# Four graph layers on one core: preparation of layer 0 in three groups of rows, table roots, moved transposes, and another PSUM bank in layer 2

## The chip, the cores and the metric

The kernel runs on one core of a Trainium2 chip. The metric is the device time of one execution in microseconds (us). Times are given as the median of several runs. The profile shows one execution of its own, and all durations in this text come from it.

The engines of the core run beside each other, each through its own queue of instructions in order: TensorE (PE, with its weight loads PEld), VectorE (DVE), ScalarE (ACT), GpSimd (POOL) and SyncE (SP, here only for DMAs). An instruction that waits holds up all that is queued behind it on its engine.

## What is computed

x is 4096 rows of 64 numbers, adj a 4096x4096 matrix of zeros and ones with some 4 ones a row. Four layers follow, each of the form x = x + layer(h, adj), with h the layer-normalized rows of x cut at zero.

```python
def lorentz_linear(x, W, b, scale):
    h = x @ W.T + b
    time = sigmoid(h[:, :1]) * exp(scale) + 1.1
    xn = h[:, 1:]
    s = (time * time - 1.0) / clip(sum(xn * xn), 1e-08)
    return concatenate([time, xn * sqrt(s)])
# layer 0
h = lorentz_linear(h_in, W, b, scale); q = lorentz_linear(h, Wq, ...); k = lorentz_linear(h, Wk, ...)
att = adj * sigmoid((2 + 2 * (qm @ k.T)) / att_scale + att_bias)   # qm: q with its first column negated
support = att @ h;  out = support / sqrt(|inner product of support|)
# layer 1: out = w @ (h @ weight) + bias, w weighs each row's last 100 neighbours by powers of 0.5
# layer 2: out = 1 - 0.1 h - 0.01 sum(h * (adj @ h), 1)
# layer 3: out = relu([h, (adj @ h) / degree] @ W.T)
```

## The kernel before

**Tiling.** The 4096 rows lie as 32 tiles (`NT`) of 128 partitions. Sums are taken over 8 blocks (`NIB`) of 512 output rows; a block has 16 units (`NG`), each of two row tiles. The blocks of layer 0 run from 7 down to 0. `adjt` is read twice. Once it comes as masks: 128 loads on POOL's queue (`load_masks`, L175), one for each unit, which turn float32 into one byte and stay in SBUF for all four layers. Once it is read to check that it holds zeros and ones only (`check`, L355 and L352 on SP's queue, L356 on DVE). The checks are spread over the whole kernel as work between other work.

**Before layer 0's sums** (`before0`, `first_rows_and_block`, L500 to L1047). Rows are prepared in groups, `ROWS = ((16, 16), (0, 16))`: first row and count in tiles of 128. A group passes through a chain, in halves of 8 (`HR`). Mean (L532, DVE), centring (L539), squares (L544, ACT), variance (L549), reciprocal root (L554 and `newton`, L481: one start value and three steps of three instructions, all on DVE), product with the root (L558). Then it is transposed on PE (L580), copied on ACT (L595), multiplied with W on PE (L628; L620 adds the bias rows that `bias_rows` makes on POOL, L388 to L397), and copied out (L650). `factors` (L714) then takes the sigmoid of the first column (L664), squares (L673), norms (L698) and `ratio` (L704: three instructions around a `newton`). L745 writes the finished rows h into `fb`. The same again for q and k together: transposes, L628, copy L771, `factors` with twice the columns, L792 for k and q. k is transposed into `kt` (L580, L595), q in `queries_turned` (L859) and `queries_laid` (L869, four ACT copies into `qt`).

The order of all this on each engine, together with block 7's units, is set by a planner, `Listing` (L399). Every part has an engine, a cost in us, what it comes after, and at times a due time `at`. `plan` places the parts greedily; `run` tries 2500 random changes of priority and keeps one whenever the time of the last part is not longer than the best so far. The last part counts on every engine, the 40 mask loads on POOL included, of which load n (from 0) has the due time 2.2 * max(n - 5, 0). Where the plan has PE idle, `fill` puts in matmuls on nothing (L1039) of 0.215 us each, and 50 of them ahead of PE's first part.

**Layer 0's sums** (L1049 to L1101). Work goes in rounds of 4 units; the block after the first has rounds of 4, 4, 3 and 3 (`first`, L1068). In a round, each unit gets `scores` on PE (L920, into one of three PSUM tiles of two banks), `sigmoids` on ACT (L933), `masked` on DVE (L944), a mask load, perhaps a check, and one `step()` of the jobs that are queued (L307). After the units of the round, PE adds up the units of the round before (`gather`, L951). The first unit of a round of 4 writes its sigmoids to SBUF, which frees its PSUM tile; the others write in place, and the tile is free when DVE has read it. When a block is summed, `rows0` (L882) becomes a job: transpose on PE (L231, third step), copy on ACT (L237), then a long chain on POOL, ACT and DVE (root on POOL, L260 to L263) up to layer 1's rows (`norm`, L266, and `split`, L242). `queries(ib - 1)` (L874) transposes the next block's q at its seventh call, between the third and the fourth unit of a block's last round, and lays it out one unit later.

**Layers 1 to 3** (L1265 to L1536). Layer 1 counts on PE (L1235, L1245), turns counts into weights on ACT (L1261) and DVE (L1259) and multiplies (L1273). Layers 2 and 3 multiply the masks with the rows (L1345); every 4 products are one beat, with a `step()` and perhaps a check. `rows2` (L1385) is the job of a finished block of layer 2: copy out (L215), transpose (L231) into PSUM bank 3 (L1392), copy (L237), sums, normalization, transposes (L1410, bank 4), products with layer 3's weights (L1422) into banks 3 and 4, copies from there (L1430, L1431). The one-buffer PSUM tile "pr" of the pool `pm` serves the transposes of layer 0 and the products of `rows1` (L1146) in layer 1; in layer 3 it serves one small product (L1136).

## Time and profile before

| what | value |
|---|---|
| median of 3 runs | 599.48 us (599.21 to 599.6) |
| the profiled execution | 599.52 us, span 597.7 us, clock 0.997 |
| PE, DVE, ACT, POOL busy | 579.2, 484.2, 335.7, 238.5 us |
| first score matmul (L920) | at 49.32 us |
| end of block 7's sum | 84.25 us |
| end of block 6's sum | 118.2 us |
| end of layer 0 | 298.7 us |
| layer 2 from, layer 3 from | 461.1 us, 528.5 us |
| end | 597.7 us |

The span runs from the first to the last instruction; 1.8 us of the profiled execution lie around it. The page gives busy times; the chain of waits tells what released each step; the table by stage gives the busy time of each engine in a stretch; the timeline lists instructions in order, with the idle time before each and what ended it.

### The profile page before, as it was taken

The numbers are of one execution on the slowest core, as the hardware profiler recorded it, in microseconds if no ns is written. First come the engines' busy times: TensorE is split into PE (matmuls) and PEld (weight loads), VectorE is DVE, ScalarE is ACT, GpSimd is POOL, SyncE is SP. The second block draws the span as 40 slices with busy tenths as digits, with TensorE's granted clock in tenths as the row PEclk, the third lists the DMA queues.
The fourth block names the chain that finished last, engine by engine and source line by source line (L and its number), as shares of the span: only waits on it lengthen the run. The fifth ranks groups of instructions, "written<-read, shape, count | busy, mean of one in ns | idle before, by whom it ended". The sixth has DMA issues, their size and how long they took to land.

```text
span 597.7 us, 9243 instructions
## 1 busy us (share of the span) xinstructions
PE 579.2 (97%) x3135; PEld 237.4 (40%) x3135; DVE 484.2 (81%) x941; ACT 335.7 (56%) x541; POOL 238.5 (40%) x459
## 2 busy tenths in 40 slices
PE   8899999899999999899999999999998999899995
PEld 3563333233333333233343343343443544454553
DVE  5878677699999997999966878979887769987753
ACT  1568665767676765666527677767765014431221
POOL 7534204456767676744344401001010315462252
PEclk9999999999999999999999999999999999999998
DMA  9995902799999998973182545546556476546921
GB/s 140 145 105 43 105 10 20 77 141 148 161 153 162 148 154 154 133 149 98 43 316 73 177 155 193 164 158 192 163 177 200 152 253 205 169 148 193 322 85 42
DMA packets 43016, 87.04 MB, mean 146 GB/s; under 512 B 5136, under 2 KB 22032, under 8 KB 42960
## 3 DMA queue, kind: packets, MB, share of 16 engines
q1 hardware_dynamic: 23808, 68.40, 34.9%
q0 software_dynamic: 18720, 17.57, 31.6%
q10 hardware_dynamic: 432, 0.40, 0.3%
q8 instruction: 26, 0.43, 0.3%
q14 instruction: 30, 0.25, 0.1%
HBM read 135.63 MB, written 1.05 MB: 229 GB/s over the span
## 4 chain that ended last, share of the span: by engine, by line
PE 86%; DVE 5%; ACT 3%; issue 2%; POOL 2%; DMA 2%; ACTq 0%; DVEq 0%; POOLq 0%
PE acc L1345 19%; PE ps L920 17%; PE acc L951 17%; PE acc L1273 10%; PE cnt L1235 9%; PE cnt L1245 3%; PE many L1168 2%; PE pt L231 2%; PE idle L1039 2%; DVE att L944 1%; PE pr L1148 1%; DMA vec<-vecs_dram 1%; PE pn L1422 1%; ACT qt L869 1%; PE ps_q L628 1%
## 5 line engine op out<-in xcount | busy, mean ns | idle before, releaser
L356 DVE SCALAR_TENSOR_TENSOR ckw<-ckw 128x1024 f32<-128x1024 f32 x98 | 124.8, 1281 | 5.6 <-DMA ckw<-adjt_dram 5.3
L920 PE MATMUL ps<-qt,kt 64*128 64x512 f32 x512 | 125.2, 613 | 3.7 <-DVE att L944 3.4
L951 PE MATMUL acc<-att,fb 128*64 128x512 f32 x512 | 118.3, 600 | 0.0
L1261 ACT ACTIVATE w<-cnt 128x512 int16<-128x512 f32 x176 | 93.1, 597 | 42.8 <-PE cnt L1245 42.3
L944 DVE TENSOR_TENSOR att<-ps,mask 128x1024 f32<-128x1024 f32 x84 | 101.1, 1219 | 9.8 <-ACT ps L933 8.9
L933 ACT ACTIVATE ps<-ps,att_c,att_a 128x1024 f32<-128x1024 f32 x84 | 95.7, 1173 | 10.0 <-PE ps L920 6.9
L933 ACT ACTIVATE att<-ps,att_c,att_a 128x1024 f32<-128x1024 f32 x44 | 52.2, 1203 | 53.4 <-PE ps L920 52.8
L175 POOL DMA_DIRECT2D mask<-adjt_dram x128 | 70.2, 560 | 19.7 <-DMA mask<-adjt_dram 17.5
L920 PEld LDWEIGHTS ps<-qt,kt 64*128 64x128 f32 x512 | 44.1, 185 | 74.7 <-DVE att L944 21.4
L1259 DVE TENSOR_SCALAR w<-cnt 128x512 int16<-128x512 f32 x80 | 53.6, 686 | 22.9 <-PE cnt L1245 22.4
L944 DVE TENSOR_TENSOR att<-att,mask 128x1024 f32<-128x1024 f32 x44 | 56.0, 1288 | 17.2 <-ACT att L933 16.8
L1235 PE MATMUL cnt<-mask,after 128*128 128x512 fp8e4 x256 | 66.3, 379 | 2.1 <-DVE w L1259 1.6
L1273 PE MATMUL acc<-w,s2a 128*128 128x512 bf16 x256 | 66.5, 382 | 0.1
L951 PEld LDWEIGHTS acc<-att,fb 128*64 128x64 f32 x512 | 33.3, 136 | 79.4 <-issue 71.4
L275 POOL TENSOR_TENSOR xc<-x_sb,st 128x256 f32<-128x256 f32 x24 | 19.1, 794 | 108.5 <-DVE st L272 55.0
L1345 PE MATMUL acc<-mask,s2a 128*128 128x512 fp8e4 x256 | 57.8, 379 | 0.0
L1345 PE MATMUL acc<-mask,s2b 128*128 128x512 fp8e4 x256 | 57.7, 379 | 0.0
L260 POOL TENSOR_TENSOR rs_a<-rs_y 128x4 f32<-128x4 f32 x48 | 16.8, 351 | 81.4 <-DVE rs_y L256 72.2
L356 DVE SCALAR_TENSOR_TENSOR ck<-ck 128x512 f32<-128x512 f32 x60 | 44.9, 748 | 0.2 <-DMA ck<-adjt_dram 0.2
L1235 PEld LDWEIGHTS <-after 128*128 128x128 bf16 x256 | 24.8, 99 | 31.0 <-issue 3.4
L1345 PEld LDWEIGHTS <-s2b 128*128 128x128 f16 x256 | 25.0, 98 | 27.5 <-issue 0.8
L1345 PEld LDWEIGHTS <-s2a 128*128 128x128 f16 x256 | 24.6, 98 | 27.3
(196 smaller groups left out, 604.1 us busy)
## 6 DMA issues: line engine op xcount, KB each, us to landing
ckw<-adjt_dram SPq DMA_DIRECT2D x98, 512.0 KB, 3.4
mask<-adjt_dram POOLq DMA_DIRECT2D x128, 128.0 KB, 9.0
ck<-adjt_dram SPq DMA_DIRECT2D x60, 256.0 KB, 5.4
x_sb<-x_dram SPq DMA_DIRECT2D x4, 256.0 KB, 8.0
out_dram<-y POOLq DMA_DIRECT2D x6, 128.0 KB, 2.2
out_dram<-y ACTq DMA_DIRECT2D x2, 128.0 KB, 2.1
w_sb<-wts_dram SPq DMA_DIRECT2D x2, 80.0 KB, 7.7
vec<-vecs_dram ACTq DMA_DIRECT2D x1, 130.5 KB, 6.5
```

The source lines that it names most:

```text
L175: nc.gpsimd.dma_start(out=masks[ib][:, g * CG : (g + 1) * CG, :], in_=adjt[ib, g])
L275: nc.gpsimd.tensor_tensor(xc, xr, bc(st, CI), ALU.add)
L356: nc.vector.scalar_tensor_tensor(at, at, 0.0, at, ALU.not_equal, ALU.not_equal, accum_out=odd[:, k : k + 1])
L920: nc.tensor.matmul(ps[:, c, :], kt[half, g, :], qts[ib][half, :], start=True, stop=True)
L933: nc.scalar.activation(to, ps, AF.Sigmoid, bias=att_c, scale=att_a)
L944: nc.vector.tensor_tensor(att, frm, mask, ALU.mult)
L951: nc.tensor.matmul(acc[c * D : (c + 1) * D, :], lhs[:, t, :], rhs[:, c, :], start=(at == 0), stop=(at == NG - 1), skip_group_check=True,)
L1235: nc.tensor.matmul(cnt, after, masks[ib][:, t, :], start=True, stop=True, skip_group_check=True)
L1259: nc.vector.tensor_scalar(w, cnt, 0.0, None, ALU.max)
L1261: nc.scalar.activation(w, cnt, AF.Relu)
L1273: nc.tensor.matmul(accs[ib], both(s2a, t), w, start=(t == NT - 1), stop=False, skip_group_check=True,)
L1345: nc.tensor.matmul(acc, both(s2, t), masks[ib][:, t, :], start=(t == 0), stop=(t == NT - 1), skip_group_check=True,)
```

## The change

1. **Three groups.** `ROWS = ((24, 8), (8, 16), (0, 8))`, with start times of 6.6, 9.5 and 13.0 in the plan; `bias_rows` costs 8.1 there instead of 3.8. The queue of SP gets the first group's x (one DMA where there were two), the weights, then the other three x DMAs.
2. **Roots of the normalization** by ACT's Sqrt table (L285's form: one ACTIVATE for a group, then one reciprocal on DVE) instead of `newton`. A Sqrt on a spare number behind the Exp of the setup loads the table early. A Sigmoid on the same number comes after the Sqrt of all three groups, and all first sigmoids of h come after that.
3. **Roots in `ratio`** by `root`, a start value and two steps of mean form (reciprocal, product with a, sum) instead of `newton`'s three steps.
4. **Transposes at the end of a round.** `rows0` and `queries` wait, a step at a time, for the last unit of a round. For `queries` that is the end of a block's third round, three units earlier than before; for `rows0` one unit later. In rounds of 3 the first unit too writes its sigmoids to SBUF.
5. **`split`** of the last two blocks of layer 0 leaves four steps instead of two between its halves.
6. **Layer 2's transposed sums** go to the tile "pr" instead of bank 3.

```diff
+GUESS, SHARE = 515594453.0, 0.0624625
+    tried = cpool.tile([P, 1], F32, name="tried")
+    nc.scalar.activation(tried, exp_s[:, 0:1], AF.Sqrt)
...
-        ROWS = ((16, 16), (0, 16))
+        ROWS = ((24, 8), (8, 16), (0, 8))
...
-        def split(h, s2, rows):
+        def split(h, s2, rows, steps=2):
             nc.gpsimd.tensor_scalar(s2[:, rows, 0, :], h, 1.0 / STEP, None, ALU.mult)
-            yield
-            yield
+            for _ in range(steps):
+                yield
...
-        def newton(v, tag, m):
...
+        def root(y, a, tag):
+            z, q = (small(f"n{b}{tag}", "", pro, a.shape[1]) for b in "zq")
             nc.vector.tensor_scalar(
+                z.bitcast(I32), a.bitcast(I32), 0.5, GUESS, ALU.mult, ALU.add
             )
+            for share, to in ((SHARE, z), (0.25, y)):
+                nc.vector.reciprocal(q, z)
+                nc.vector.scalar_tensor_tensor(q, q, share, a, ALU.mult, ALU.mult)
+                nc.vector.tensor_tensor(to, q, z, ALU.add)
...
-            def roots(_):
-                nc.vector.tensor_scalar(v.va, v.va, 1.0 / D, EPS, ALU.mult, ALU.add)
-                v.rs = newton(v.va, f"x{gr}", R)
+            def rooted(_):
+                v.rs = numbers("rs")
+                nc.scalar.activation(v.rs, v.va, AF.Sqrt, bias=eps, scale=1.0 / D)
+            def inverted(_):
+                nc.vector.reciprocal(v.rs, v.rs)
...
-            at = (6.6, 14.5)[gr]
+            at = (6.6, 9.5, 13.0)[gr]
...
-            rs = add("DVE", 2.4, roots, *va)
+            sq = add("ACT", 0.25, rooted, *va)
+            tables.append(sq)
+            rs = add("DVE", 0.2, inverted, sq)
...
                     nc.vector.tensor_scalar(rr, rr, 1e-8, None, ALU.max)
-                    nc.vector.scalar_tensor_tensor(rr, t2, -1.0, rr, ALU.add, ALU.mult)
-                    y = newton(rr, f"{name}{gr}", R * n)
-                    nc.vector.scalar_tensor_tensor(rr, t2, -1.0, y, ALU.add, ALU.mult)
+                    nc.vector.reciprocal(rr, rr)
+                    nc.vector.scalar_tensor_tensor(t2, t2, -1.0, rr, ALU.add, ALU.mult)
+                    root(rr, t2, f"{name}{gr}")
...
-                return add("DVE", 2.8, ratio(name, n), tm, *rr)
+                return add("DVE", 2.25, ratio(name, n), tm, *rr)
...
         def queries(ib):
-            for _ in range(6):
+            for _ in range(3):
+                yield
+            while not edge[0]:
                 yield
             pt = pm.tile([P, CI, P], F32, tag="pr", name=f"pq_{ib}{sfx}")
...
             yield
-            yield
+            while not edge[0]:
+                yield
             pt = turned(asb, None, tag)
...
-            yield from split(h, s2a, rows)
+            yield from split(h, s2a, rows, 4 if ib < 2 else 2)
...
-            bias = add("POOL", 3.8, lambda _: bias_rows(), at=6.5)
+            bias = add("POOL", 8.1, lambda _: bias_rows(), at=6.5)
...
+            table = add("ACT", 1.5, lambda _: nc.scalar.activation(tried, tried, AF.Sigmoid), *tables)
+            for part in flats:
+                part.after += (table,)
+                table.then.append(part)
...
-                for ib, g in todo[k : k + size]:
+                for n, (ib, g) in enumerate(todo[k : k + size]):
+                    edge[0] = n == size - 1
                     ps = scores(ib, g)
-                    if size == 4 and not now:
+                    if size > 2 and not now:
...
+            edge[0] = True
...
-            pt = turned(asb, 3, tag)
+            pt = turned(asb, None, tag)
```

(`flats` holds each group's first ACT part of `factors` for h, the sigmoid L664.)

More of the change, by code (lines that the diff above doesn't have):

```diff
@@ L479, in run @@
                     part.emit(part)
-        def newton(v, tag, m):
-            y, a = (small(f"n{b}{tag}", "", pro, m) for b in "ya")
+        def root(y, a, tag):
+            z, q = (small(f"n{b}{tag}", "", pro, a.shape[1]) for b in "zq")
             nc.vector.tensor_scalar(
-                y.bitcast(I32), v.bitcast(I32), -0.5, 1597463007.0, ALU.mult, ALU.add
+                z.bitcast(I32), a.bitcast(I32), 0.5, GUESS, ALU.mult, ALU.add
             )
-            for _ in range(3):
-                nc.vector.tensor_tensor(a, y, y, ALU.mult)
-                nc.vector.scalar_tensor_tensor(a, a, -0.5, v, ALU.mult, ALU.mult)
-                nc.vector.scalar_tensor_tensor(y, a, 1.5, y, ALU.add, ALU.mult)
-            return y
+            for share, to in ((SHARE, z), (0.25, y)):
+                nc.vector.reciprocal(q, z)
+                nc.vector.scalar_tensor_tensor(q, q, share, a, ALU.mult, ALU.mult)
+                nc.vector.tensor_tensor(to, q, z, ALU.add)
+        tables, flats = [], []
         TURN = ("pm", "pa")
@@ L726, in factors @@
                 sg = add("ACT", 0.26, flat, *frm_parts)
+                if n == 1:
+                    flats.append(sg)
                 tm = add("DVE", 0.2 + 0.2 * n, time_sums(name, n, scales), sg)
@@ L852, in model @@
         spare, turn = [], [0]
+        edge = [False]
         qts = {}
```

## The prediction

> **What bounds the kernel now.** First the page's busy times. PE works almost all the time, so time is won only where PE idles, runs matmuls on nothing, or waits.
>
> ```profile
> PE 579.2 (97%) x3135; PEld 237.4 (40%) x3135; DVE 484.2 (81%) x941; ACT 335.7 (56%) x541; POOL 238.5 (40%) x459
> ```
>
> The average hides three stages, so I took the table by stage (us, then PE, PEld, DVE, ACT, POOL busy).
>
> ```profile
> 49.30:84.25 34.95, 34.83 (x150) 10.95 (x150) 26.00 (x34) 24.20 (x30) 10.89 (x17) 1.00 0.63 57
> 84.25:123.19 38.94, 37.06 (x164) 12.81 (x166) 28.38 (x47) 27.58 (x30) 18.35 (x48) 1.00 0.47 45
> 153.42:183.74 30.32, 30.32 (x136) 10.36 (x138) 28.38 (x48) 21.19 (x25) 20.91 (x46) 1.00 1.03 157
> 516.98:523.34 6.36, 5.84 (x36) 3.12 (x34) 6.09 (x14) 2.92 (x9) 2.95 (x5) 1.00 0.52 164
> ```
>
> From 49.3 us PE is full; before it, its work is mostly L1039, which is nothing. A block of layer 0 is full on PE at 30.3 us, with DVE behind it by 1.9 us only. Layer 2 has DVE at 6.09 of 6.36 us. Then I followed the first group's chain in the timeline.
>
> ```profile
> 12.06 0.34 DVE L554 TENSOR_SCALAR va<-va 128x16 f32<-128x16 f32 x1
> ...
> 15.08 0.69 DVE L558 SCALAR_TENSOR_TENSOR xc<-xc,nyx 128x512 f32<-128x512 f32 x1
> ...
> 22.54 1.28 ACT L664 ACT_TABLE_LOAD   x1
> ...
> 26.27 0.17 DVE L708 TENSOR_SCALAR rrh<-rrh 128x16 f32<-128x16 f32 x1
> ...
> 28.99 1.29 DVE L745 TENSOR_TENSOR fb<-t,rrh 128x512 f32<-128x512 f32 x2
> ```
>
> The normalization's root takes 3.0 us (12.06 to 15.08, fold's instruction and slow ones within), the ratio 2.7 us (26.27 to 28.99), the second ratio 2.9 us (41.02 to 43.95, 32 columns). The first score comes at 49.32.
>
> **Groups and roots: the start.** First the DVE sum. The two normalization roots go (3.0 and 2.3 us); three reciprocals of 0.2 us come: -4.7. A ratio was 13 instructions, at a step of 0.21 us (16 columns) or 0.225 us (32), and is now 10, three of them reciprocals. Rows for those: 0.17 us at 4 columns (L289), 0.25 at 16 (L1218), so some 0.007 us a column, 0.2 at 8 and 0.36 at 32. A ratio is then 2.1, 2.3 or 2.75 us at 8, 16 or 32 columns. But there are six of them instead of four: 2.1+2.3+2.1 for h and 2.3+2.75+2.3 for q and k, 13.9 against 11.2: +2.7. A third set of small instructions adds 1.0. DVE's 63.1 us up to 84.25 become some 62.1: its work hardly falls, only the first chain gets shorter.
>
> That chain, with 8 rows: mean from 7.6, centred 9.15, squares 9.85, variance 10.55, Sqrt (L285: 0.32) and reciprocal 11.15, normalized 11.85. There the gain stops for a while: PE's 50 matmuls on nothing end at 15.4, and the bias rows on POOL at 14.8. So transposed 16.05, copied 16.7, multiplied 18.1 (0.39 and 1.0), out at 18.75. The sigmoid must wait for the Sqrt of the third group: DVE is full from 7.6 with 3.0 us for the first group, 4.1 for the second, 2.2 for the third, so 17, and the table (1.28) is there at 18.5. Both meet. Sigmoid 19.0, squares 19.6, norms 20.3, ratio 22.4, rows 23.1, first column 23.3, transposed and copied 24.7, multiplied 26.2, out 27.3, sigmoid and squares 28.7, norms 29.4, ratio 31.7, k and q 33, q transposed and laid (1.5) and the other copy 35.5. With the other groups' instructions between I take the first score at 37 instead of 49.3.
>
> PE needed 34.9 us from there to the end of block 7's sum; 37 + 35 = 72. But the first group holds only 4 units (7.5 us of PE). The second group's k needs, in DVE's order, 46.5, the third's 65.6 with the masks between (1.25 us each): PE starves for 2 and 3 us. So 77 instead of 84.25: **-7.3 us**. DVE's idle time would fall from 13.8 (84.25 - 7.3 - 63.1) to 7.6 us. The planner speaks for the same place: its last mask load is due at 74.8 and costs 0.56, so no plan counts as better than 75.4 of its own us, and it has no reason to finish PE sooner. Bounds: 72 (nothing starves) and 82 (third group's k another 5 us late), -12 to -2.
>
> The added Sqrt table load is hidden: from 7.5, when Exp is done, to 8.8, ahead of the squares at 9.2; and PE is held until 15.4 anyway. The before shows 1.32 us from the end of the copy (22.51) to the sigmoid (23.83), the load within.
>
> The Trainium skill (ScalarE: Activation LUTs, What ACT_TABLE_LOAD costs) speaks against this edit: it gives 1.28 us for a load and 1.38 more for a drain at each switch. By it the Sqrt load would end at 10.2 and the sigmoid come 1.4 us later. The trace has the 1.28 and no drain, so I leave it out of the sum.
>
> On POOL, three halves of q instead of two (1.9 and 1.1 us) stand among the mask loads; masks came every 1.25 us from 21 us on, and 18 are enough by 60, so nothing waits. Price if it did: one load, 1.25.
>
> **Block 6 (84 to 123).** Its rounds without waiting are 2.2 us shorter than measured. The one long wait is PE from 111.9 to 113.5 for DVE, which came late because four qt copies (106.7 to 108.2) stood between ACT's sigmoids, and then the constants (110.6 to 112.2) on DVE. The copies now come a round earlier, where there are no checks, and the first unit of rounds of 3 goes to SBUF: **-1.6**, bounds -2.2 and 0.
>
> **Transposes at ends of rounds.** The chain of waits shows plain rounds and those with a transpose inside the scores:
>
> ```profile
> 153.42 3.58 PE acc L951 x16
> 157.00 3.63 PE ps L920 x16
> 160.64 3.58 PE acc L951 x16
> 164.22 2.78 PE ps L920 x12
> 167.37 1.06 PE ps L920 x4
> 168.42 3.58 PE acc L951 x16
> ```
>
> Sum to sum 7.22 us plain, 7.78 with q's two transposes (+0.56), 8.01 with the four of sums (+0.79). Once in the before q's stand at a round's end (100.46): there scores to sums took 3.14 against 2.77 (104.42), +0.37. So a place between is worth 0.19. Five q's and seven sums move: -2.3. Against it: the copies that follow now stand behind the first sigmoid of a round (qt 1.5 us, pt 0.59) where ACT was idle during the sums before. DVE then waits some 0.75 us for the second sigmoid in a round with three checks, and PE some 0.45 for DVE's fourth product, as DVE has only 1.9 us to spare in a block. Six blocks, half of them with such a wait: +1.3. **-1.0**, bounds -2.3 and +4.
>
> The wait near 237 (POOL's loads held for 2.1 us, then L275, then ACT) has no cause the profile names; I leave it, 2.2 either way. `split`'s two steps: the last block's chain has 20 steps of 23 before its rows are needed, so nothing.
>
> **Layer 2.**
>
> ```profile
> 508.74 0.71 PE L1422 MATMUL pn<-wxn_sb,ht 64*128 64x128 f32 x8
> ...
> 509.97 0.66 PE L231 MATMUL pt<-ident,asb 128*128 128x128 f32 x4 [0.52 <-ACT v L1431]
> ```
>
> Bank 3 holds pn until ACT has copied it, and pt waits. In the chain of waits that is 0.47 us, and pt takes 0.66 instead of 0.44 after a stop: 0.69 each, at 503.6, 510.0, 516.3 and 522.7: -2.8. "pr" is free: its last user in layer 1 is at 467, and sums follow each other by five beats. What is late next is DVE: 6.1 us of work in periods of then 5.7, 0.4 a period behind, 1.7 us in all, while its normalized rows (L297, done at 511.3) are now 1.8 us ahead of PE's use (513.06). **-2.3**, bounds -2.8 and -0.3.
>
> **Sum.** -7.3 - 1.6 - 1.0 - 2.3 = -12.2 on the profiled 599.52, which is the median within 0.04: 587.3. Between block 6 and layer 2 the work is tied to units, not to time, so an earlier start stays.
>
> **Rivals.**
> - *The start is bound by DVE after all* (its work does not fall; six ratios): block 7 ends at 82; 592.3. Chance 0.17.
> - *Nothing starves*: PE dense from 37, end at 72; 582.3. Against it: four units only in the first group. 0.15.
> - *Layer 2 is DVE's* (6.09 of 6.36 busy): -0.3 there, 589.3. 0.10.
> - *A table switch costs twice its row*: 1.28 more ahead of the first sigmoid, 588.6. The row speaks against it; beside it stands the page above. 0.05.
> - *Slower: ACT's detour reaches PE in full.* The two copies (2.09 us) and the check queued behind the late product (0.75) cost 2.84 a block, 17 us over six blocks, and block 6 gains nothing: 17 - 2.3 - 7.3 - 2.3 = +5, 604.6. For it: DVE's 94%. Against: mask products have nearly a round until their sum. It decides from (7.3+2.3+2.3+1.6)/6 = 2.25 us a block. 0.07.
> - Forecast, as summed: 0.46.
>
> **Range.** 582 to 594 leaves out the slower case, half of "nothing starves" and an edge. A measurement of this kernel tells 0.2% (1.2 us) from no change: faster 0.89, same 0.04, slower 0.07.
>
> **What would show it.** First score near 37, block 7's end near 77, L1039 fewer before it. A table load near 7.5 and one near 17. Rounds of layer 0 at 7.6 with transposes and DVE over 95%; PE waiting on L944 in a block's fourth round would be the slower case. In layer 2 pt right behind pn, no wait on L1431; if instead ph or pn waits for DVE or ACT, DVE took the gain. The forecast is wrong if the third group's k comes after 70, or a block takes over 31 us.

## The result, and the profile after

The changed kernel takes 597.68 us (median of 7 runs, 595.4 to 598.73) beside 599.4 us; the ratio is 0.9961 (0.9946 to 0.9977). It is faster by 1.7 us, and not by 12.2; 587.3 was forecast and 582 to 594 given as the range. The profiled execution took 597.85 us, its span 596.1 us.

The page's first lines show little: PE is busy for 3.4 us less, since 101 instead of 123 matmuls on nothing run, and is at 97% as before.

```profile
span 596.1 us, 9196 instructions
...
PE 575.8 (97%) x3115; PEld 237.8 (40%) x3115; DVE 481.8 (81%) x935; ACT 338.4 (57%) x549; POOL 243.5 (41%) x460
```

The stages tell more. A stage ends here where ACT begins to copy the finished sum (L214, for layer 1 L220; five lines less in the kernel before), so each length is one subtraction of two starts.

| stage, us | before | after | difference | forecast |
|---|---|---|---|---|
| first score | 49.32 | 43.02 | -6.3 | -12.3 |
| end of block 7's sum | 84.29 | 82.65 | -1.6 | -7.3 |
| block 6 | 33.95 | 32.80 | -1.15 | -1.6 |
| blocks 5 to 0 | 180.52 | 180.23 | -0.3 | -1.0 |
| layer 1 | 161.86 | 165.57 | **+3.7** | 0 |
| rest (layers 2, 3) | 137.1 | 134.85 | -2.2 | -2.3 |

Two rows need a second look. The row of blocks 5 to 0 holds a wait at its end. PE ends the last of these sums 179.2 us after block 6's (180.5 in the kernel before), which is 1.3 us less. But ACT's copy of it then begins 1.10 us after PE's last product instead of 0.05, behind squares that wait for POOL. First the kernel before, then the changed kernel:

```profile
298.76 0.59 ACT L209 COPY asb<-acc 128x512 f32<-128x512 f32 x1 [1.56 <-PE acc L951]
```

```profile
295.36 0.42 ACT L283 ACTIVATE sq<-xc 128x256 f32<-128x256 f32 x1 [5.86 <-POOL xc L280]
295.68 0.57 ACT L214 COPY asb<-acc 128x512 f32<-128x512 f32 x1
```

And of the 3.7 us of layer 1, 0.6 lies in its first quarter (52.64 against 52.03 us) and 3.1 in its last (39.63 against 36.54).

The table by stage of the changed kernel (stretch, us, then PE, PEld, DVE, ACT, POOL busy, clock), for the start, block 6, a later block and a period of layer 2:

```profile
43.02:82.54 39.52, 37.91 (x151) 12.45 (x151) 30.64 (x41) 27.50 (x36) 16.04 (x23) 0.96 0.74 67
82.54:115.40 32.86, 32.23 (x146) 11.28 (x144) 24.07 (x42) 23.46 (x26) 14.08 (x37) 1.00 0.43 38
176.15:207.08 30.93, 30.32 (x136) 10.52 (x134) 28.23 (x49) 21.08 (x25) 21.21 (x46) 1.00 1.00 153
509.24:515.01 5.77, 5.77 (x40) 3.13 (x36) 5.56 (x14) 2.81 (x9) 3.63 (x4) 1.00 0.56 182
```

In the start the stretch from the first score is 4.6 us longer than before (39.52 against 34.95), and its clock is 0.96; PE idles only 1.6 us in it. A later block is 30.93 long and PE idles 0.6 in it, where it was full at 30.3. Layer 2's period fell from 6.36 to 5.77 us.

**All runs.** Each line is one kernel: its median, its ratio to the kernel before, and stages of its one profile. The kernel before has runs near 599.2 us with a mean clock of 0.996 to 0.999 and runs near 600.9 us with 0.993 to 0.995, so each ratio is taken to its runs of the same session on the same chip.

| kernel | median | ratio (95%) | first score | block 7 ends | block 6 | 5 to 0 | layer 1 |
|---|---|---|---|---|---|---|---|
| before | 599.4 | 1 | 49.32 | 84.29 | 33.95 | 180.52 | 161.86 |
| after | 597.68 | 0.9961 (0.9946-0.9977) | 43.02 | 82.65 | 32.80 | 180.23 | 165.57 |
| e1 | 595.6 | 0.9931 (0.9914-0.9947) | 42.84 | 81.75 | 32.80 | 180.54 | 163.53 |
| e2 | 599.12 | 0.9992 (0.9981-1.0003) | 42.60 | 81.52 | 32.57 | 182.14 | 164.95 |
| e3 | 598.06 | 0.9975 (0.9962-0.9989) | 45.45 | 84.38 | 33.73 | 181.93 | 162.62 |
| e4 | 597.22 | 0.9964 (0.9949-0.9980) | 49.19 | 84.16 | 33.94 | 180.53 | 161.62 |
| e5 | 600.2 | 1.0006 (0.9984-1.0028) | 45.46 | 84.37 | 32.38 | 180.27 | 169.10 |
| e6 | 598.37 | 0.9980 (0.9968-0.9992) | 39.47 | 86.11 | 32.80 | 180.32 | 162.52 |
| e7 | 600.48 | 1.0012 (1.0002-1.0022) | 52.44 | 88.32 | 32.79 | 180.30 | 162.70 |
| e8 | 602.54 | 1.0044 (1.0027-1.0061) | 43.84 | 83.34 | 32.38 | 181.39 | 169.37 |
| e9 | 596.75 | 0.9956 (0.9940-0.9971) | 43.40 | 83.08 | 32.80 | 180.21 | 163.44 |
| e10 | 595.59 | 0.9939 (0.9926-0.9952) | 43.35 | 83.13 | 32.80 | 180.30 | 162.31 |
| e11 | 601.25 | 1.0021 (1.0010-1.0032) | 49.74 | 88.87 | 32.80 | 180.22 | 162.60 |
| e12 | 594.19 | 0.9911 (0.9898-0.9924) | 44.84 | 80.39 | 32.81 | 180.10 | 162.91 |
| e13 | 595.55 | 0.9923 (0.9904-0.9941) | 43.15 | 82.77 | 33.94 | 179.97 | 162.15 |
| e14 | 605.15 | 1.0092 (1.0072-1.0111) | 49.18 | 84.14 | 32.80 | 180.29 | 166.01 |
| e15 | 593.9 | 0.9897 (0.9879-0.9915) | 45.02 | 80.58 | 32.80 | 180.30 | 163.32 |
| e16 | 593.05 | 0.9886 (0.9865-0.9906) | 44.18 | 81.12 | 32.79 | 180.24 | 162.27 |
| e17 | 592.4 | 0.9881 (0.9858-0.9903) | 44.14 | 81.09 | 32.57 | 180.23 | 161.91 |

### The profile page after: what moved, and what is told of

The parts are those of the page before. It is cut to its first block, busy times and chain, and to the rows that moved or that the text cites. A ratio compares the mean times of both kernels' runs of the same rounds, so it can differ in the third digit from the quotient of the medians.

```text
span 596.1 us, 9196 instructions
## 1 busy us (share of the span) xinstructions
PE 575.8 (97%) x3115; PEld 237.8 (40%) x3115; DVE 481.8 (81%) x935; ACT 338.4 (57%) x549; POOL 243.5 (41%) x460
## 3 DMA queue, kind: packets, MB, share of 16 engines
HBM read 135.63 MB, written 1.05 MB: 229 GB/s over the span
## 4 chain that ended last, share of the span: by engine, by line
PE 76%; DVE 9%; POOL 5%; ACT 4%; issue 3%; DMA 2%; SPq 0%; DVEq 0%; POOLq 0%; ACTq 0%
PE acc L1370 19%; PE ps L938 14%; PE acc L969 14%; PE acc L1298 9%; PE cnt L1260 8%; PE cnt L1270 3%; PE idle L1062 3%; DVE att L962 3%; PE pt L236 2%; DMA ckw<-adjt_dram 2%; POOL mask L180 1%; ACT ps L951 1%; PE pr L1173 1%; ACT att L951 1%; POOL rs_a L265 1%
## 5 line engine op out<-in xcount | busy, mean ns | idle before, releaser
L962 DVE TENSOR_TENSOR att<-ps,mask 128x1024 f32<-128x1024 f32 x82 | 98.4, 1216 | 8.3 <-ACT ps L951 8.2
L951 ACT ACTIVATE ps<-ps,att_c,att_a 128x1024 f32<-128x1024 f32 x82 | 93.4, 1176 | 1.5 <-PE ps L938 1.3
L951 ACT ACTIVATE att<-ps,att_c,att_a 128x1024 f32<-128x1024 f32 x46 | 54.7, 1202 | 56.9 <-PE ps L938 56.7
L938 PEld LDWEIGHTS ps<-qt,kt 64*128 64x128 f32 x512 | 46.5, 187 | 80.2 <-issue 32.2
L962 DVE TENSOR_TENSOR att<-att,mask 128x1024 f32<-128x1024 f32 x46 | 57.5, 1263 | 17.2 <-ACT att L951 17.1
L280 POOL TENSOR_TENSOR xc<-x_sb,st 128x256 f32<-128x256 f32 x24 | 19.9, 831 | 113.3 <-DVE st L277 59.5
L265 POOL TENSOR_TENSOR rs_a<-rs_y 128x4 f32<-128x4 f32 x48 | 18.3, 380 | 69.5 <-DVE rs_y L261 66.9
L361 DVE SCALAR_TENSOR_TENSOR ck<-ck 128x512 f32<-128x512 f32 x60 | 42.9, 714 | 0.3 <-DMA ck<-adjt_dram 0.3
L1260 PEld LDWEIGHTS <-after 128*128 128x128 bf16 x256 | 25.0, 100 | 33.4 <-issue 6.5
```

Of the source, the lines that this page charges most:

```text
L265: nc.gpsimd.tensor_tensor(a, y, y, ALU.mult)
L361: nc.vector.scalar_tensor_tensor(at, at, 0.0, at, ALU.not_equal, ALU.not_equal, accum_out=odd[:, k : k + 1])
L938: nc.tensor.matmul(ps[:, c, :], kt[half, g, :], qts[ib][half, :], start=True, stop=True)
L951: nc.scalar.activation(to, ps, AF.Sigmoid, bias=att_c, scale=att_a)
L962: nc.vector.tensor_tensor(att, frm, mask, ALU.mult)
L1260: nc.tensor.matmul(cnt, after, masks[ib][:, t, :], start=True, stop=True, skip_group_check=True)
```

## Experiments on the start

**The same start in eight profiles.** Up to the end of block 7's sum, e2, e3, e5, e8, e9, e10 and e13 issue the changed kernel's instructions in its order on PE, DVE and ACT; only later ones were edited. Their first scores lie between 42.60 and 45.46, their sum's ends between 81.52 and 84.38. So this start gains between -0.1 and 2.8 us, and the changed kernel's own profile, with 1.6, is one of the better ones. (The kernel before, e4 and e14 share their start too, and end the sum within 0.15 us of each other.) The chain of waits of the changed kernel names what shifts it:

```profile
1.58 12.94 PE idle L1062 x50
14.96 1.51 PE idle L1062 x7
...
17.52 3.13 PE idle L1062 x14
```

PE's first transposes follow the 50 matmuls on nothing without a wait, at 13.9 to 15.2 us, and ACT stands still for 5.95 us ahead of the copy of these transposes, with the second group's squares behind it. In six of the eight profiles the first score comes 28.7 to 28.8 us after the first transposes; in e3 and e5 it is 30.3, with the granted clock at 0.50 for 3.4 us from 27.7 on. What fewer matmuls on nothing would bring was not tested.

**e6, the first group alone first.** The first score came 6 us later than forecast. DVE's timeline of the changed kernel shows where: the first group's second squares are ready (norms at 31.28), and then DVE works on the second group's h.

```profile
31.28 0.68 DVE L710 TENSOR_REDUCE rrq<-sqq 128x8 f32<-128x504 f32 x1
31.88 0.17 DVE L719 TENSOR_SCALAR rrh<-rrh 128x16 f32<-128x16 f32 x1
...
34.19 1.29 DVE L758 TENSOR_TENSOR fb<-t,rrh 128x512 f32<-128x512 f32 x2
35.40 1.25 DVE L710 TENSOR_REDUCE rrq<-sqq 128x8 f32<-128x504 f32 x2
36.58 0.17 DVE L719 TENSOR_SCALAR rrq<-rrq 128x16 f32<-128x16 f32 x1
```

From 31.88 to 35.40 the 16 columns of `rrh` belong to the second group; the first group's own ratio (`rrq`) begins at 36.58. e6 makes the others wait:

```diff
+                first = asked_first if n == 1 and gr else []
+                done = add("DVE", 2.25, ratio(name, n), tm, *rr, *first)
+                if n == 2 and not gr:
+                    asked_first.append(done)
```

> The changed kernel, with one dependency more in the planner: the ratio of h of the second and third group comes after the first group's ratio of q and k, so that DVE serves the first chain alone. As the prediction had it (the end of block 7's sum is the first score plus PE's work): the first score comes near 39.5 instead of 43.0, and the sum ends near 79 to 80, 594.5 in all. Rival (the end hangs on when DVE has finished the second group's k and the mask products; an early first score only gives PE an earlier wait): first score near 39.5 to 40, but PE starves after the first units until k of the other groups comes, and the sum ends at 85 to 86, later than now; the time is 600 to 601.

The first score came at 39.47, 3.5 us earlier, and block 7's sum ended at 86.11, 3.5 us **later**. The rival's mechanism holds: from 39.47 on PE had four units and then waited. Its time does not: 598.37 and not 600 to 601, since layer 1 took 3 us less than in the changed kernel.

**e16, another order of the same work.** The planner's random search starts from 2 instead of 1.

```diff
-                draw = random.Random(1)
+                draw = random.Random(2)
```

> The changed kernel with the other start of the planner's random search and nothing else. Theory (the order in which DVE serves the three groups sets the end of block 7's sum, not the first score): the first score comes 1.5 to 2 us later, at 44.5 to 45, and still block 7's sum ends 1.5 us or more earlier, at 81; 596. Rival (the first score sets it): the sum ends 1.5 to 2 us later, at 84.5, 599.5.

The first score came at 44.18, within the spread above, the sum's end at 81.12, below it, and the median is 593.05. Of the 4.8 us by which e16's span is shorter than the changed kernel's, 1.5 lie ahead of the sum's end and 3.3 in layer 1, which this edit does not touch. Counted from PE's first transposes, the sum ends 66.0 us later in the two profiles with e16's start (e16 and e17) and 67.5 to 69.2 us later in the eight of the changed kernel's: the order is worth 1.5 us or more. DVE's k of the second group (8 units) shows what is different. First the changed kernel, then e16:

```profile
59.80 0.68 DVE L805 TENSOR_TENSOR kr<-tq,rrq 128x512 f32<-128x512 f32 x1
...
62.67 0.68 DVE L805 TENSOR_TENSOR kr<-tq,rrq 128x512 f32<-128x512 f32 x1
```

```profile
46.34 2.15 DVE L805 TENSOR_TENSOR kr<-tq,rrq 128x512 f32<-128x512 f32 x2
```

In e16 the second group's k follows the first's by 6 us. In the changed kernel the third group's k (4 units, 43.69) went first, and the 8 units came 13 to 16 us later than in e16. How this makes the stretch longer is only in part seen: PE idles 1.9 us in e16's (36.87, busy 34.97) and no more in the changed kernel's (39.52, busy 37.91). Of the 2.9 us that it is busy for longer, the halved clock (e1) explains 1.7; the rest has no wait that names it.

**e7 and e11, one half of the start each.** e7 puts back two groups; e11 keeps three groups and puts back the normalization's `newton`, without the Sqrt table.

```diff
-        ROWS = ((24, 8), (8, 16), (0, 8))
+        ROWS = ((16, 16), (0, 16))
...
-            at = (6.6, 9.5, 13.0)[gr]
+            at = (6.6, 9.5)[gr]
```

> The changed kernel with two groups of 16, as before the change; the roots by table and by mean form, and all else, stay. As the prediction had it (the groups bring the early first score and with it most of the 7.3 us): first score near 48, and block 7's sum ends 5 us later, at 87.5, 602.7 in all. Rival (DVE's work up to the end counts, and two groups have two ratios less): first score near 48, but the sum ends at 82.5 to 83.5, within 1 us of three groups, 598 in all; then the groups give nearly nothing, and the shorter roots give what the start gained.

```diff
-            sq = add("ACT", 0.25, rooted, *va)
-            tables.append(sq)
-            rs = add("DVE", 0.2, inverted, sq)
+            rs = add("DVE", 2.4, roots, *va)
```

> The changed kernel with three groups, but the normalization's roots on DVE by the three steps of before, and no Sqrt table in the start; the shorter roots in ratio stay. As the prediction had it (the table takes 4.7 us off DVE, with three groups some 7): the first score comes 3 to 7 us later, and block 7's sum ends at 86 to 88 instead of 82.6, 602 in all. Rival (the first sigmoid waits for the Sqrt of all three groups, from 18.1 to 20.6, and this gives back what the table saves): first score near 43 to 44, the sum ends at 83 to 84, 599.

Block 7 ends at 88.32 and 88.87: each half alone is 4 to 4.6 us slower than the kernel before, and together they are 1.6 faster. My rivals fell in both. But e7 does not price the groups. Its edit also plans the second group from 9.5 us on, where the kernel before has 14.5. DVE takes that group's means ahead of the first group's variance and waits 1.97 and 1.31 us for their x. PE stands idle meanwhile, and its granted clock is then 0.50 from 18.1 to 28.3:

```profile
18.99 1.94 PE L592 MATMUL pt_h<-ident,xc 128*128 128x128 f32 x8 [5.05 <-DVE xc L568]
```

The first transposes come 3.1 us later than in the kernel before (18.99 and 15.92), and from there the first score takes as long in both (33.4 us). In e11 six ratios and three `newton`s lie on DVE. Each of these kernels has another planned order, so part of the difference is the order's (e16: 1.5 us).

**e1, the clock after PE's wait.** Ahead of the first score PE waits 1.66 us, and the granted clock then falls:

```profile
41.00:43.00 2.00, 0.35 (x4) 0.12 (x2) 1.73 (x9) 1.95 (x7) 0.00 (x0) 1.00 0.76 71
43.00:45.00 2.00, 1.98 (x5) 1.77 (x7) 1.82 (x6) 1.57 (x4) 1.27 (x1) 0.54 0.01 1
45.00:47.00 2.00, 2.00 (x6) 0.58 (x4) 0.89 (x4) 1.36 (x3) 1.89 (x4) 0.61 0.25 10
47.00:49.00 2.00, 2.00 (x12) 0.91 (x13) 1.73 (x3) 2.00 (x4) 0.00 (x0) 1.00 1.09 97
```

```diff
-                if part.form == "scores":
-                    v.filling = None
-                    return
-                for _ in range(int((part.idle - 0.1) / 0.215) if v.filling else 50):
+                first = part.form == "scores"
+                count = int((part.idle - 0.1) / 0.215) if v.filling else 50
+                for _ in range(8 if first else count):
```

> The changed kernel, with eight matmuls on nothing (0.215 us each) ahead of its first score matmuls, where PE stood idle from 41.35 to 43.02 and the granted clock then was 0.50 to 0.71 for 3.7 us. Theory (the idle 1.66 us brought the clock down, and the slow matmuls pushed all that follows): the clock stays at 1.00 from 43 to 47, the first eight score matmuls take 1.99 us instead of 3.93, block 7's sum ends at 82.5 instead of 84.25, and the time falls by 1.7 from 597.7 to 596.0. Rival (the end of block 7's sum is set by how DVE feeds PE, and the slow clock only filled time in which PE would have waited): the clock is 1.00, but the sum ends at 84 all the same, PE waits more for L938 and L962 before 65, and the time stays at 597.7. Third case: the clock has nothing to do with the idle time, and it falls again.

The clock stayed at 1.00. From first score to sum's end it took 38.9 instead of 39.6 us: 0.7, not 1.7, because PE then waits for ACT and DVE (0.67 and 0.81 us). The eight profiles of the same start agree: 38.9 us in the three whose clock is 1.00 in this stretch, 39.5 to 39.8 in the five where it falls. The rival is right for more than half. The median fell by 2.1; the rest is layer 1's end (below), which this edit does not touch.

## Experiments on the moved transposes

In a block of layer 0 PE's sums start so far apart (us; first the round after the sums' transpose):

| kernel | round 1 | 2 | 3 | 4 | sum |
|---|---|---|---|---|---|
| before | 7.22 | 7.78 (queries) | 7.22 | 8.09 (sums) | 30.3 |
| after | 7.59 (queries) | 7.22 | 7.44 | 8.69 (sums) | 30.9 |
| e2: sums back | 7.59 | 7.21 | 8.00 | 8.01 | 30.8 |
| e3: queries back | 7.22 | 7.79 | 7.22 | 9.11 | 31.3 |
| e8: sums' copy early | 7.59 | 7.21 | 8.00 | 7.81 | 30.6 |
| e5: both copies early | 7.59 | 7.22 | 7.51 | 8.06 | 30.4 |

The queries' place is worth what was forecast (7.78 to 7.59). Then rounds 3 and 4 get longer. Against this stands one round of the kernel before, the fourth from 236.7 on, of 10.2 us with PE waiting 1.38 us for DVE: the changed kernel has no such round. By PE's sums, blocks 5 to 0 take 30.8, 30.2, 30.6, 30.6, 32.5 and 25.9 us before and 30.1, 30.3, 30.9, 30.9, 30.9 and 26.0 after. In the changed kernel's chain of waits, the stretch before PE's stop at 209.27 runs through POOL, ACT and DVE:

```profile
194.85 1.05 POOL rs_a L265
...
199.36 1.09 POOL sup L918
...
202.82 1.08 POOL mask L180 x2
203.91 0.65 POOL xc L280
...
204.90 1.17 ACT ps L951
206.10 1.22 DVE att L962
...
207.99 1.24 DVE att L962
209.27 1.99 PE ps L938 x8
```

and ACT's timeline has the link between POOL and the sigmoid:

```profile
201.54 1.17 ACT L951 ACTIVATE ps<-ps,att_c,att_a 128x1024 f32<-128x1024 f32 x1
204.58 0.42 ACT L283 ACTIVATE sq<-xc 128x256 f32<-128x256 f32 x1 [1.87 <-POOL xc L280]
204.90 2.26 ACT L951 ACTIVATE ps<-ps,att_c,att_a 128x1024 f32<-128x1024 f32 x2
```

The squares stand between two sigmoids and wait 1.87 us for POOL's chain, which began later because the sums' copy did; the mask loads stand ahead of L280 on POOL.

**e2 and e3, one move undone each.**

```diff
             yield
-            while not edge[0]:
-                yield
+            yield
             pt = turned(asb, None, tag)
```

> The changed kernel, with the transposes of the finished sums back at their third step, one unit earlier; the queries stay at the end of the third round. Theory (the later transpose pushes the chain on POOL, the ACT squares of L283 then wait 1.87 us for POOL, and ACT's sigmoid, DVE and PE follow): three blocks of layer 0 that took 30.9 us from sum to sum are back at 30.3 and pay 0.2 for a transpose within the scores, so 30.5 each, and the time falls by about 1.3 to 596.4. Rival (the copies of the queries behind the first sigmoid of a round are the cause): the blocks stay at 30.9 and pay 0.2 more, 598.9.

```diff
-            for _ in range(3):
-                yield
-            while not edge[0]:
+            for _ in range(6):
                 yield
             pt = pm.tile(
```

> The changed kernel, with the queries' transposes and copies back within a block's fourth round; the transposes of the sums stay at the end of the round. Theory (the transposes of the sums are the cause): blocks still at 30.9 with ACT's squares waiting for POOL, and 0.2 more each for the place within the scores, and block 6 loses some 1 us of its gain: 599 to 600. Rival (the queries' copies are the cause): blocks at 30.4, 595.5 or less.

Undoing the sums' move takes L283's wait from 1.87 to 0.34 us and round 4 from 8.69 to 8.01, as the theory said; but round 3 then takes 8.00. So the queries' copies cost as well, and neither theory alone holds. Both kernels lose 1.7 to 1.9 us in blocks 5 to 0.

**e5, e8 and e9, the copies ahead of the sigmoids.**

```diff
             pt = turned(asb, None, tag)
-            yield
             sup = rows_tile("sup", tag)
...
             queries_turned(ib, pt)
-            yield
             queries_laid(ib, pt)
```

> The changed kernel, with the ACT copies of the transposed sums and of the queries issued in the same step as their transposes, so that they stand ahead of the next round's first sigmoid, where ACT is idle for 2.3 to 3.8 us, and not behind it. Theory (the moved transposes gained on PE what was forecast, but their copies behind the first sigmoid cost it again: the sums' copy makes the chain on POOL late, so that ACT's squares of L283 hold the third sigmoid of the fourth round for 1.87 us, and the queries' copies hold up the second): the wait of L283 goes, the rounds of a block take 7.2, 7.2, 7.6 and 7.8 us, a block 29.9 instead of 30.9, blocks 5 to 0 take 175.5 instead of 180.2, and the time falls by some 4.5 to 593. Rival 1 (DVE, with 28.4 us of work in a block and checks besides, cannot follow): blocks at 30.3 with PE waiting for L962, 595.5. Rival 2 (the transposes at the ends cost PE by themselves): blocks stay at 30.9, 597.7.

e8 has the first of the two edits only.

> The changed kernel, with only the copy of the transposed sums issued together with its transposes; the queries' copies stay behind the next round's first sigmoid. Theory (two costs, one from each copy): the wait of L283 for POOL goes and the round with the sums' transposes falls from 8.7 to 7.8 us, but the fourth round stays at 7.4 to 8.0, as it did when only the queries were moved: blocks at 30.1 to 30.6, 595 to 596.5. Rival (all of it comes from the late chain on POOL): as good as with both copies, blocks at 29.9, 593.

Round 4 fell to 7.81 with the sums' copy (e8) and round 3 to 7.51 with the queries' too (e5): a block of 30.4, not 29.9. DVE's busy time is 29.04 of its 30.38 us. And the time grew. In e5 DVE waits 4.06 us for POOL's `x_sb` at layer 1's start and PE 2.8 for DVE, since rows0's chain there runs on PE's steps, not on time, and the granted clock halves twice in layer 1, for 3.4 us each time. e9 keeps the old steps for the last two blocks and starts the others' normalization one step later.

```diff
+            if ib < 2:
+                yield
...
+            for _ in range(4 if ib < 2 else 5):
+                yield
             h = yield from norm(rows, None, tag, False)
```

> The changed kernel with both copies at once, but the layer-1 end of the chain kept where it was: for blocks 7 to 2 the normalization in rows0 starts one step later, so that POOL has a unit's time more ahead of the squares of L283, and for the last two blocks the transposed sums are copied as in the changed kernel. Theory (the copies behind the first sigmoid cost the fourth and the last round; the loss with both copies at once came from the steps at layer 1's start, where DVE waited 4.06 us for POOL and PE 2.8 for DVE): L283 waits under 0.7 us in every block, the rounds take 7.2, 7.4, 7.6 and 7.8 to 8.1, no wait near 240, blocks 5 to 0 take 178 instead of 180.2, layer 1 is as in the changed kernel, and the time is 595.5 to 596. Rival (DVE sets the block at 30.4 whatever ACT does, and the wait near 240 comes back): 180, 598.

The loss at layer 1's start went, but blocks 5 to 0 took 180.21: the long round of the kernel before was back near 240 (L283 waits 2.42 for POOL there). The rival holds.

**e13 and e14, both moves.** e13 undoes the two edits above and the sigmoid to SBUF in rounds of 3; e14 adds these three to the kernel before.

> The changed kernel with both moves undone: queries and transposed sums within the rounds as before, and in rounds of 3 no sigmoid to SBUF. As the prediction had it (the moves are worth 1.6 in block 6 and 1.0 after it): 600.3. Rival (what the moves take off PE comes back as waits for ACT and DVE, since DVE has 28 to 29 us of work in a block; and the squares that wait for POOL put layer 1's first product 1.0 later): block 6 takes 33.9 instead of 32.8, blocks 5 to 0 180.5 as in the kernel before, layer 1 begins after a PE wait of 0.7 instead of 1.7: 0.4 more than the changed kernel, 598.1, or no difference that these runs can tell.

> The kernel before with the two moves alone. As the prediction had it: 596.9. Rival: block 6 gains 1.1 and the wait near 243 goes, but the blocks take 30.9 and the first product of layer 1 waits 1.7 us for the sums behind the squares: 598.5 to 599.2, within 0.2 per cent of the kernel before.

e13: block 6 +1.1, blocks 5 to 0 -0.3, layer 1's first wait 0.69 instead of 1.72, and the median 595.55, 2.1 *below* the changed kernel's, mostly for layer 1's end. e14 lost some 5 us (1.0092). In its profile it is 1.5 us ahead of the kernel before when layer 0 ends, loses 4.2 in layer 1, and 2.0 more behind the issue of the last output, which these edits do not explain. DVE shows the largest single cause:

```profile
315.07 0.69 DVE L1265 TENSOR_SCALAR w<-cnt 128x512 int16<-128x512 f32 x1 [1.21 <-PE cnt L1241]
319.64 0.94 DVE L248 SCALAR_TENSOR_TENSOR s2a<-s2a,xc 128x256 f16<-128x256 f16 x1 [3.88 <-POOL s2a L245]
```

L248 is the second half of `split`; it waits 3.88 us for POOL, with layer 1's weights behind it, and PE 2.66 for these. The granted clock is 0.50 for 3.4 us besides (from 299.5), which costs up to 1.7. e14 lacks the change's two further steps in `split`. No run adds them to e14; that they remove the wait is argued from the changed kernel, which has them and where PE waits 0.18 us for DVE in that quarter of layer 1.

## Experiments on layers 1 and 2

**e10, layer 1's end.** In the changed kernel one check load lands 5.0 us after its issue (median 3.4), DVE waits for it, PE for DVE, and the clock halves. DVE's line, then PE's table (PE is idle to 454.9):

```profile
453.04 1.22 DVE L361 SCALAR_TENSOR_TENSOR ckw<-ckw 128x1024 f32<-128x1024 f32 x1 [2.09 <-DMA ckw<-adjt_dram]
```

```profile
454.00:456.00 2.00, 1.07 (x7) 0.31 (x7) 1.56 (x5) 0.06 (x1) 0.00 (x0) 1.00 0.32 70
456.00:458.00 2.00, 2.00 (x7) 0.73 (x6) 1.74 (x3) 1.51 (x3) 0.00 (x0) 0.54 0.49 193
458.00:460.00 2.00, 2.00 (x10) 0.49 (x9) 0.36 (x1) 0.34 (x1) 0.00 (x0) 0.60 0.60 219
```

```diff
-            more[:] = pool("ck2", 1), 4
+            more[:] = pool("ck2", 1), 5
```

> The changed kernel with five buffers instead of four for the check loads of layers 1 to 3. Theory (layer 1's end is tied to time by a check load that lands late: DVE waits for it, 2.09 us in the profile, PE 3.12 us for DVE, and then the granted clock halves for 3.4 us): the load is issued one check earlier, DVE does not wait for it, PE waits 1.4 us or less near 454, the clock stays at 1.00 there, layer 1 takes 162.5 instead of 167, and the median falls by 2 to 3, to 595. Rival (the load is held by the DMA engines, not by its buffer): DVE waits as long, and the time stays at 597.7.

DVE's wait fell to 0.75, PE's to 1.64, the clock stayed at 1.00, layer 1 took 162.31, and the median 595.59, 2.1 us less (1.3 by the ratios). That is what the theory forecast, but that the fifth buffer did it is not shown. With four buffers PE waits 1.35 to 1.67 us at this place in ten profiles, those of the kernel before and of e16 among them, and 2.0 to 3.1 in six (after, e1, e2, e5, e8, e9); the three kernels with five buffers have 1.24 to 1.64. Why the load is late in some executions stays open.

**e4, layer 2's bank alone.**

```diff
-            pt = turned(asb, 3, tag)
+            pt = turned(asb, None, tag)
```

> The kernel before, with layer 2's transposed sums in the tile pr and nothing else changed. Theory (the four waits for ACT's copies out of bank 3 were in PE's way): layer 2 takes 65.2 instead of 67.4 us, and the time falls by 2.2 to 597.2. Rival (layer 2 is DVE's, or the time comes back in layer 3): layer 2 at 67 or layer 3 longer than 69.2, and the time stays at 599.2. As a third of the change's gain is 1.7, the first case means that this one line is worth more than the whole change.

597.22: 2.2 us less, all in layer 2, from one line. In its timeline pt follows pn at once:

```profile
507.78 0.72 PE L1422 MATMUL pn<-wxn_sb,ht 64*128 64x128 f32 x8
508.42 0.65 PE L231 MATMUL pt<-ident,asb 128*128 128x128 f32 x4
```

## Versions that are faster

> The changed kernel with four edits together: matmuls on nothing ahead of the first score, both copies at once with the last blocks kept, five buffers for the check loads, and another start of the planner's random search (2 instead of 1), whose order ends earlier by its own count. If each cause found so far is one of its own, the gains add: 0.7 to 2 in the start from the clock, up to 1.8 from the order, 2 in blocks 5 to 0, 2 to 3 at layer 1's end: 590 to 592. If instead layer 1 gives back what an earlier start brings, layer 0 ends near 290 but layer 1 takes over 165, and the time stays at 595.

> The best kernel so far (all four mends) without the edits of the copies: the changed kernel with matmuls on nothing ahead of the first score, the other start of the random search, and five check buffers. Theory (the copies' edits moved waits and gave nothing): as good as with them, block 7's sum ends at 80.4, blocks 5 to 0 take 180.2, and the time is within 0.6 of 594.2. Rival (they gave the 2 us that were expected of them): 596 or more.

> The changed kernel with the other order of the random search, with the transposed sums back within the rounds, and with the queries early only in block 6, where their copies otherwise meet the constants. Theory (the move pays in block 6 alone and costs in layer 1's start): block 7's sum ends at 81.1, block 6 takes 32.6, blocks 5 to 0 take 180 to 180.5, PE waits 0.7 and not 1.7 us at layer 1's start, layer 1 takes 161.7 to 162.2; 592.2, the fastest of all runs by less than 1 us. Rival (with the sums back, the queries' early copies cost in block 5 what block 6 gains, as where only the sums were put back): 593 to 594.

e12 (e1's, e9's, e10's and e16's edits) takes 594.19, e15 (the same without the copies' edits) 593.9. So the copies' edits give nothing, and the gains do not add: e16's one edit alone gives 593.05, in a profile that has neither the halved clock in the start nor the late load in layer 1. e17 has e16's order, the sums back in the rounds, and the queries early for block 5 only, which is in block 6:

```diff
+            early = ib == NIB - 3
+            for _ in range(3 if early else 6):
+                yield
+            while early and not edge[0]:
                 yield
```

It takes 592.4, 1.2% less than the kernel before (0.9881, 0.9858 to 0.9903), the fastest here; from e16 it cannot be told.

## Why the prediction was wrong

- **The start, -7.3: measured -1.6.** The step that failed is "With the other groups' instructions between I take the first score at 37": it was 43.02. I had 1.5 us for other groups' work. DVE, "full from 7.6", waited 1.34 and 1.42 us for the second group's x, ACT stood behind PE's 50 matmuls on nothing, and the sigmoid came 1.6 later than my 19.0. Then the second group's h took 3.5 us ahead of the first group's ratio, and e6 shows this term: without it the first score comes at 39.47. The other 2.5 were not taken apart by a run.
- **From the first score to the sum's end** I had 40 us, "PE needed 34.9 us from there" and 5 for starving; 39.6 were measured. That is luck: PE idled 1.6 us and not 5, and the halved clock, which the sum does not have, made PE busy for longer. An early first score does not bring an early end either: e6 moved one by -3.5 and the other by +3.5. The order in which DVE serves the groups counts. My 46.5 for the second group's k and 65.6 for the third's were e16's order (46.34 and 65.90); the kernel had them the other way round (59.80 and 62.67 for the second's two halves, 43.69 for the third's). The rival "DVE-bound after all" gave 82, and 82.65 was measured, but its mechanism is not what the trace shows: DVE's sum was 62.5, as I had it (62.1), and DVE is busy for only 30.6 of the 39.5 us. The planner's argument fell: it bounded the plan, and said nothing on which order the search finds. Neither of the two signs of being wrong came (the third group's k after 70, a block over 31 us), and the forecast was wrong all the same.
- **Roots.** A reciprocal took 0.20, 0.25 and 0.35 us at 8, 16 and 32 columns, as worked out. The loads of the table took 1.28 us, and the next ACTIVATE began 0.02 later (load at 19.22, next at 20.52). The drain of 1.38 us that the Trainium skill (ScalarE: Activation LUTs, What ACT_TABLE_LOAD costs) adds at each switch does not show, as I had it.
- **Block 6, -1.6: -1.15.** Right in cause; the constants still delay PE by 0.63 us.
- **Transposes, -1.0: -0.3.** By PE's sums it is -1.3, and the last sum's copy, 1.05 us late behind the squares, takes most of it back. The gain of 0.19 a place was right. The term that was mis-sized is ACT's detour, "half of them with such a wait: +1.3": it is 1.0 us in each of the three middle blocks (30.9, where the rounds without it give 7.6 + 7.2 + 7.2 + 7.9), and part of it comes by a way that I had not seen, through POOL. The rival of the slower case had a detour of ACT in full and too large. That the row still shows a gain is luck: the long round near 237, which I left out of the sum, is 1.5 us shorter, and no run shows why.
- **`split`, nothing: wrong.** I counted its steps and not its place on DVE's queue; e14, with the moves and without it, has 2.66 us of PE's wait there.
- **"Between block 6 and layer 2 the work is tied to units, not to time, so an earlier start stays": wrong, +3.7 us in layer 1 and 1.05 ahead of it.** The first product of layer 1 waits 1.72 instead of 0.69 us, as the last sum's copy (L214) stands behind squares that wait 5.86 us for POOL (3.15 before); this lies in the row of blocks 5 to 0. In layer 1's last quarter PE waits 3.1 us for DVE and DVE for a check load, whose landing goes by time, and the clock halves: 3.1 of the 3.7 us. The kernel before waits there too, for 1.6 us, and what made the load late is open (e10).
- **Layer 2, -2.3: -2.2** (e4 the same alone). Right, and DVE followed, at 5.56 of 5.77 us.

## What to carry to other kernels

When one engine feeds another in order, work out when the *most* of the work becomes ready, not when the first piece does; in e6 a small group that started early bought only an early wait. Where two engines are within 2 us of each other in a period of 30, do not count time taken from one as a gain: follow what the moved copies stand in front of, over POOL too, until the round closes. And a chain that runs by steps of PE's program meets different times at a change of stage: check what stands behind its waits there. Last, profile one start more than once: here it ended anywhere within 2.9 us.

## What the runs showed of the hardware

The granted clock falls to 0.50 for about 3.4 us after some waits of PE. Over the 19 profiles, from 40 us on, no wait of 1.0 to 1.5 us (18) was followed by it, 8 of 31 between 1.5 and 2.0, and 6 of 8 over 2.0 (not after 2.55 in e9 and 2.66 in e14). The same wait of 1.66 us ahead of the first score had it in five profiles and not in three. So the length of the wait does not decide alone: ahead of 40 us, a wait of 0.78 us near 27 was followed by it in e3 and e5 and not in the seven other profiles with the same start, and one of 5.05 us (e7) by 10.24 us at 0.50. The Trainium skill (TensorE: Matmul & The Clock Gate, What's actually happening) says that the activity is watched in a free-running window of 3.4 us, which agrees with the length and would explain the chance. The advice of the Trainium skill to keep gaps under some 3 us (same page, Why this matters for your kernels) is too generous here.

Three of DVE's mask products took 5.19 us, 1.73 each instead of 1.22, from 54.68 on, while POOL multiplied two halves of q (from 54.91, 1.94 us each). Work given to POOL to spare DVE slowed DVE beside it.
